# State space layer: B and C from one product, C copied by DMA, and dt in array quarters with one transpose

## The chip, the cores and the metric

The kernel runs on one core of one Trainium2 chip. The metric is the device time of one execution in microseconds (us); lower is better. Before the change three executions took 1665.72, 1667.54 and 1668.49 us; the median, 1667.54 us, is the time before.

The core has five engines that work side by side, each on its own list of instructions in order: TensorE (PE, matrix products and transposes; its weight loads are shown apart as PEld), VectorE (DVE), ScalarE (ACT), GpSimd (POOL) and SyncE (SP, here only an issuer of transfers). Transfers run on 16 DMA engines. Products go to PSUM, which has banks of 128 partitions by 512 float32, and are copied from there into SBUF.

## The reference

Two layers over x of 4 sequences, 1024 tokens, 256 features, all in float32. Layer 0 is a state space mixer and a feed-forward network, layer 1 a linear attention and a mixture of experts; each of the four parts ends in a residual sum and a layernorm. The part that the change touches is the projection of the state space mixer, cut from the reference:

```
def ssd_forward(x, W_xproj, dt_bias, A_log, D):
    dtBC = x @ W_xproj.T                       # 256 features -> 2 + 64 + 64
    dt = dtBC[..., :NHEADS]                    # one step size for each of 2 heads
    Bm = dtBC[..., NHEADS:NHEADS + D_STATE]    # D_STATE = 64
    Cm = dtBC[..., NHEADS + D_STATE:]
    dt = jax.nn.softplus(dt + dt_bias)
    A = -jnp.exp(A_log)
    Xh = x.reshape(b, T, NHEADS, HEADDIM) * dt[..., None]
    y = ssd_minimal_discrete(Xh, A * dt, Bm, Cm, T)    # B, C shared by both heads
    return y + x * D_full
```

The mixer itself weighs the products of C (of a later token) with B (of an earlier one) by a decay exp of the sum of A dt between the two, and multiplies the result with dt x. The kernel does this by tiles of 128 tokens and carries a state of 64 x 128 per head from tile to tile, which C reads (the reference computes a sequence at once; the result is the same).

## The kernel before

**Tiles and stages.** The 4096 tokens are eight blocks of 512: block i belongs to sequence i // 2, and an odd block continues its even one. Each block has four tiles of 128 tokens. x is loaded twice, as rows (x0 to x7, tokens on partitions) and turned (xt0 to xt7, features on partitions). `two_layers` (L74) is the whole kernel; `ssd_block` (L265) makes one block of the state space mixer, `ffn_block` (L418) one of the feed-forward network, `attn_front` and its fellows half a block of the attention, and shared and routed jobs the experts.

**One state space block.** `project(0)` (L272) multiplies xt with weights whose 128 columns are B (64), dt (2) and padding, so that bc0 has B on partitions 0 to 63 and dt on 64 and 65, with 512 tokens along; `project(1)` does it with C twice, so that bc1 has C on both halves of the partitions. Each is two products of 128x128 with 128x512 (the profile counts each of these instructions twice), and an ACT copy out of PSUM (L279). `steps` (L281) turns bc0 by four transposes (L285), copies B and dt (128 x 264) to dtb by ACT (L287), and computes the step sizes with a softplus in some twenty small DVE operations (L293 to L306) and one ACT exp (L295). The last of them gives a (L306). `sums` (L309) makes cumulative sums of a by three products with constant masks (L316) and their exp, and the first `shade` (L327): on POOL am (L332), the mask scaled by a, and bs (L334), B scaled by step and decay. `scores` (L336) multiplies B by C of each tile (L341; 64 partitions are contracted) and masks on DVE (L343). For each tile j, `weights(j)` (L347) makes the decays (product L350, exp L352) and weighs the scores (DVE L355); `step(j)` (L361) makes y (L371), the state's addition s (L380) and the reading of the old state by C (L385: head 0 with C and state on partitions 0 to 63, head 1 on 64 to 127), and DVE sums them up. After the fourth tile comes the layernorm.

**Who sets the order.** PE's order is fixed by a planner at build time: every stage is a `Task` (class at L231) with a cost, a rank, waits after other tasks, and PSUM banks of one of two pools (six banks for the state space and the attention, two for the feed-forward network). `trace_tasks` takes the task that can begin first and, of equals, that of lowest rank; its planned times decide the order alone, while on the chip each instruction runs when semaphores allow. The even blocks come first, the odd ones follow as their even ones end, and the feed-forward blocks fill the gaps in the order 0, 2, 1, 3 to 7. The other engines are ordered by the framework's scheduler. The tasks of the front part of a block are

```
t_b = Task(lambda: project(0), 1.8, r, [(before, 0.0)], 0, 1)
t_c = Task(lambda: project(1), 1.8, r + 0.02, [(t_b, 0.0)], 0, 1)
t_d = Task(steps, 0.5, r + 0.01, [(t_b, 1.7)], 0, 1)
t_c = Task(scores, 0.9, r + 0.02, [(t_c, 1.7)], 0, 1, 2.0)
t_u = Task(sums, 0.5, r + 0.03, [(t_d, 7.0)], 0, 1, 1.0)
```

**Loads.** SP issues the loads up to the router's weights ahead of anything else (L118 to L135): the projection's weights wx, xt0, small vectors, xt2, xt4, xt6, x0, x2, x4, x6, col, the feed-forward weights w1 and w2, then xt1, x1, xt3, x3 and so on, and the attention's weights; then zero fills of the routed slots (L1062). Transfers reuse a limited set of semaphores, so that an issue can wait for an earlier transfer with the same one.

Of the kernel before, what the change touches and what calls it, by code (L numbers as in the profile page):

```python
# [23 lines left out]
F32 = mybir.dt.float32  # L24
# [6 lines left out]
P = 128  # L31
NB, T, D = 4, 1024, 256
TB = 512
NT = TB // P
# [5 lines left out]
VW = 32  # L40
# [33 lines left out]
def two_layers(ctx: ExitStack, tc: tile.TileContext, x, xT, vecs, cols, wx, w1, w2, wqkv, wout, om, rw, moe, out):  # L74
# [29 lines left out]
    w2_sb = wkf.tile([P, HID0 // P, D], F32, name="w2_sb")  # L104
    ssd_pool = tc.tile_pool(name="l0s", bufs=1, side="right")
    wk0 = ssd_pool.__enter__()
    wx_sb = wk0.tile([P, KC, 2, P], F32, name="wx_sb")
    xts = [wk0.tile([P, KC, TB], F32, tag=f"xt{i // 2}", name=f"xt{i}", bufs=2) for i in range(NBLK)]
    attw_pool = tc.tile_pool(name="attw", bufs=1)
    wkw = attw_pool.__enter__()  # L110
# [152 lines left out]
    def ssd_block(i, wk):  # L263
# [6 lines left out]
        def small(tag):  # L270
            return sm.tile([P, NT, NH1], F32, tag=f"ssd{b}_{tag}", name=f"ssd_{tag}{i}")

        def project(s):

            ps = bank(f"ps_bc{i}_{s}", 0)
            for k in range(KC):
                nc.tensor.matmul(ps, wx_sb[:, k, s, :], xts[i][:, k, :], start=(k == 0), stop=(k == KC - 1))
            v.bc[s] = wk.tile([P, TB], F32, tag=f"bc{b}_{s}", name=f"bc{i}_{s}")
            nc.scalar.copy(v.bc[s], ps)  # L279

        def steps():  # L281

            ps = bank(f"ps_dtb{i}", 0)
            for j in range(NT):
                nc.tensor.transpose(ps[:, j * P : (j + 1) * P], v.bc[0][:, j * P : (j + 1) * P], ident)  # L285
            dtb = v.dtb = wk.tile([P, NT, NST + NH1], F32, tag=f"dtb{b}", name=f"dtb{i}")
            nc.scalar.copy(dtb, ps.rearrange("p (j n) -> p j n", j=NT)[:, :, : NST + NH1])  # L287

            z, e, w, w2, q, dt, a = v.chain = [small(t) for t in ("z", "e", "w", "w2", "q", "dt", "a")]
            bias = vec0[:, _VEC["dt_bias"]].unsqueeze(1).to_broadcast([P, NT, NH1])
            nc.vector.tensor_add(z, dtb[:, :, NST:], bias)  # L293
            nc.vector.scalar_tensor_tensor(e, z, -1.0, z, ALU.mult, ALU.max)
            nc.scalar.activation(e, e, AF.Exp, scale=-1.0)  # L295
            nc.vector.tensor_scalar_add(w, e, 2.0)
            nc.vector.reciprocal(w, w)
            nc.vector.tensor_mul(w, w, e)
            nc.vector.tensor_mul(w2, w, w)
            nc.vector.tensor_scalar_mul(q, w2, 1.0 / 17.0)  # L300
            for n in (15.0, 13.0, 11.0, 9.0, 7.0, 5.0, 3.0):
                nc.vector.scalar_tensor_tensor(q, q, 1.0 / n, w2, ALU.add, ALU.mult)
            nc.vector.scalar_tensor_tensor(q, q, 1.0, w, ALU.add, ALU.mult)
            nc.vector.tensor_scalar_max(z, z, 0.0)
            nc.vector.scalar_tensor_tensor(dt, q, 2.0, z, ALU.mult, ALU.add)
            nc.vector.tensor_mul(a, dt, neg_a.unsqueeze(1).to_broadcast([P, NT, NH1]))  # L306
# [20 lines left out]
        def shade(j):  # L327

            v.am[j] = wk.tile([P, NH1, P], F32, tag=f"am{b}", name=f"am{i}_{j}", bufs=2)
            v.bs[j] = wk.tile([P, NH1, NST], F32, tag=f"bs{b}", name=f"bs{i}_{j}", bufs=2)  # L330
            for h in range(NH1):
                nc.gpsimd.tensor_scalar_mul(v.am[j][:, h, :], mask_le, v.chain[6][:, j, h : h + 1])  # L332
            for h in range(NH1):
                nc.gpsimd.tensor_scalar_mul(v.bs[j][:, h, :], v.dtb[:, j, :NST], v.dts[:, j, h : h + 1])  # L334

        def scores():  # L336

            ps = bank(f"ps_sc{i}", 0)
            for j in range(NT):
                tok = slice(j * P, (j + 1) * P)  # L340
                nc.tensor.matmul(ps[:, tok], v.bc[0][:NST, tok], v.bc[1][:NST, tok], start=True, stop=True)  # L341
            v.sc = wk.tile([P, NT, P], F32, tag=f"sc{b}", name=f"sc{i}")
            nc.vector.tensor_mul(  # L343
                v.sc, ps.rearrange("p (j l) -> p j l", j=NT), mask_le.unsqueeze(1).to_broadcast([P, NT, P])
            )
# [15 lines left out]
        def step(j):  # L361


            state = states[b]
            tok = slice(j * P, (j + 1) * P)
            first, last = i % 2 == 0 and j == 0, i % 2 == 1 and j == NT - 1
            ps_y, ps_s = (bank(f"ps_{n}{i}_{j}", 0) for n in "ys")
            halves = [slice(h * NST, (h + 1) * NST) for h in range(NH1)]
            past = [ps_y[:, D : D + P], ps_s[:, P : 2 * P]]
            for h in range(NH1):  # L370
                nc.tensor.matmul(  # L371
                    ps_y[:, h * P : (h + 1) * P],
                    v.wt[j][:, h, :],
                    x_i[:, j, h * P : (h + 1) * P],
                    start=True,
                    stop=True,
                )
            if not last:
                for h in range(NH1):
                    nc.tensor.matmul(  # L380
                        ps_s[halves[h], :P], v.bs[j][:, h, :], x_i[:, j, h * P : (h + 1) * P], start=True, stop=True
                    )
            if not first:
                for h in range(NH1):
                    nc.tensor.matmul(past[h], v.bc[1][halves[h], tok], state[halves[h], :], start=True, stop=True)  # L385
            if not last:
                new = wk.tile([P, P], F32, tag=f"state{b}", name=f"state{i}_{j}", bufs=2)
                if first:
                    nc.vector.tensor_copy(new, ps_s[:, :P])
                else:  # L390
                    nc.vector.scalar_tensor_tensor(new, state, v.end[:, j : j + 1], ps_s[:, :P], ALU.mult, ALU.add)
                states[b] = new
            for h in range(NH1):
                xh = x_i[:, j, h * P : (h + 1) * P]
                nc.vector.scalar_tensor_tensor(
                    xh, xh, d_plus[:, h : h + 1], ps_y[:, h * P : (h + 1) * P], ALU.mult, ALU.add
                )
                if not first:
                    nc.vector.scalar_tensor_tensor(xh, past[h], v.ex[:, 0, j, h : h + 1], xh, ALU.mult, ALU.add)
            if j == NT - 1:  # L400
                layernorm(i, by_act=True)

        before = ssd_end.get(i - 1) if i % 2 else None
        r = b + 0.4 * (i % 2)
        t_b = Task(lambda: project(0), 1.8, r, [(before, 0.0)], 0, 1)
        t_c = Task(lambda: project(1), 1.8, r + 0.02, [(t_b, 0.0)], 0, 1)
        t_d = Task(steps, 0.5, r + 0.01, [(t_b, 1.7)], 0, 1)
        t_c = Task(scores, 0.9, r + 0.02, [(t_c, 1.7)], 0, 1, 2.0)
        t_u = Task(sums, 0.5, r + 0.03, [(t_d, 7.0)], 0, 1, 1.0)
        t_s = None  # L410
        for j in range(NT):
            s = r + 0.04 + 0.01 * j
# [787 lines left out]
def _layout(g):  # L1200
# [7 lines left out]

    w = _rows(g["L0_attn_W_xproj"].T)
    dt, bm, cm = w[:, :, :NH1], w[:, :, NH1 : NH1 + NST], w[:, :, NH1 + NST :]  # L1210
    pad = np.zeros((P, KC, P - NST - NH1), w.dtype)
    wx = np.stack([np.concatenate([bm, dt, pad], axis=2), np.concatenate([cm, cm], axis=2)], axis=2)

    def expert(w1, w3, w2):
        return np.concatenate([_rows(w1.T), _rows(w3.T), _rows(w2.T).reshape(P, 2, HID)], axis=1)
# [41 lines left out]
```

## Time and profile before

The profile is of one execution of 1667.01 us; the span from its first to its last instruction is 1665.3 us.

| | us | share of the span |
|---|---|---|
| profiled execution | 1667.01 | |
| its span | 1665.3 | |
| PE busy | 1530.3 | 92% |
| PE weight loads busy | 1000.9 | 60% |
| DVE busy | 745.2 | 45% |
| ACT busy | 606.0 | 36% |
| POOL busy | 479.5 | 29% |
| state space projection (L277) on PE | 31.6 | 2% |
| its four transposes per block (L285) on PE | 4.9 | 0.3% |
| ACT copies of bc (L279) and dtb (L287) | 9.2 and 3.0 | 0.7% |

The mean granted TensorE clock is 0.960 of full speed. Busy times of different engines overlap. The state space blocks lie in the first tenth of the span: the first product is at about 5 us, the last tile of block 7 at 164 us. A stretch with everything busy says nothing of which engine the others wait for; the waits and the stretches between them do. In rows of instructions, the columns are start, length, engine, line, operation, output<-inputs, shapes and count, and in brackets the idle time of the engine before and the one that ended it. In rows of groups, they are line, engine, operation, output<-inputs, shapes and count, then busy us and mean ns of one, then idle us before and who ended them.

### The profile page before, as it was taken

To read this page: it belongs to the slowest core of one execution; us is meant where nothing else is said; L and a number is where in the kernel's file an instruction comes from. 1 tells how busy PE (TensorE), PEld (TensorE's weight loads), DVE (VectorE), ACT (ScalarE), POOL (GpSimd) and SP (SyncE) were. 2 spreads that over 40 slices of the span, in tenths; PEclk is the share of its full clock that TensorE was granted. 3 is DMA by queue.
4 is the path that set the end of the run, shared out by engine and by line. 5 is a ranking of instruction groups with operands and counts; after the bars stand their busy time and mean duration, and the time that the engine had idled before them with its cause. 6 is when DMAs were issued, how large, how long until landed. Compare 5 with 4: busy or idle time off the path is not lost.

```text
span 1665.3 us, 25514 instructions
## 1 busy us (share of the span) xinstructions
PE 1530.3 (92%) x9680; PEld 1000.9 (60%) x9680; DVE 745.2 (45%) x2264; ACT 606.0 (36%) x1065; POOL 479.5 (29%) x509
## 2 busy tenths in 40 slices
PE   8999898989999989999999972989999999999887
PEld 5566565757676757657667641456666666665554
DVE  6877734756566538454544410112222222222665
ACT  2545463464635365354565200112222222221221
POOL 6623243443323434233322077030000000003541
PEclk9999999999999999999999995899999999999999
DMA  9400000000000002001000382031111111111331
GB/s 346 184 1 1 1 1 1 14 1 1 14 2 14 1 14 89 1 14 35 6 14 27 124 324 104 29 111 45 48 45 45 45 47 46 46 41 57 117 105 64
DMA packets 53207, 92.60 MB, mean 56 GB/s; under 512 B 6624, under 2 KB 37472, under 8 KB 51552
## 3 DMA queue, kind: packets, MB, share of 16 engines
q1 hardware_dynamic: 44496, 67.89, 11.5%
q0 software_dynamic: 6864, 19.41, 3.6%
q10 hardware_dynamic: 1728, 3.67, 0.6%
q8 instruction: 80, 1.31, 0.3%
q14 instruction: 39, 0.32, 0.1%
HBM read 52.93 MB, written 38.01 MB: 55 GB/s over the span
## 4 chain that ended last, share of the span: by engine, by line
PE 71%; DVE 12%; ACT 8%; issue 4%; POOL 3%; DMA 1%; SPq 1%; DVEq 0%; ACTq 0%; POOLq 0%
PE ps_ge L944 15%; PE ps_g L882 12%; PE ps_ye L966 7%; PE ps_e L900 7%; PE ps_f L442 5%; PE ps_h L430 5%; PE ps_sc L600 3%; PE ps_o L636 3%; PE ps_gT L959 2%; PE ps_qk L486 2%; PE ps_k L622 1%; PE ps_v L511 1%; PE ps_p L548 1%; ACT L433 1%; PE ps_xe L935 1%
## 5 line engine op out<-in xcount | busy, mean ns | idle before, releaser
L944 PE MATMUL ps_ge<-w,xeT 128*128 x568 | 258.2, 598 | 0.7 <-ACT xeT L937 0.6
L882 PE MATMUL ps_g<-xTs,w 128*128 128x512 f32 x512 | 229.6, 602 | 6.1 <-ACT sl L890 6.1
L993 POOL DMA_INDIRECT y<-yg,slot x64 | 62.8, 981 | 453.5 <-ACT sl L890 404.0
L900 PE MATMUL ps_e<-w,gT 128*128 128x256 f32 x512 | 132.1, 407 | 58.9 <-issue 46.7
L882 PEld LDWEIGHTS ps_g<-xTs,w 128*128 128x128 f32 x512 | 96.6, 192 | 120.1 <-issue 108.2
L944 PEld LDWEIGHTS ps_ge<-w,xeT 128*128 128x128 f32 x568 | 103.3, 192 | 104.8 <-issue 103.8
L900 PEld LDWEIGHTS ps_e<-w,gT 128*128 128x128 f32 x512 | 102.3, 203 | 88.0 <-issue 59.6
L430 PE MATMUL ps_h<-xT,w_sb 128*128 128x512 f32 x256 | 129.6, 650 | 22.3 <-ACT hT L433 12.9
L954 DVE TENSOR_TENSOR ge<-se,ps_ge 128x512 f32<-128x512 f32 x71 | 48.8, 687 | 222.9 <-PE ps_ge L944 222.9
L966 PE MATMUL ps_ye<-w2e,geT 128*128 x568 | 134.4, 380 | 0.0
L891 DVE TENSOR_TENSOR gT<-sl,ps_g 128x512 f32<-128x512 f32 x64 | 43.9, 686 | 196.5 <-PE ps_g L882 159.9
L442 PE MATMUL ps_f<-w_sb,hT 128*128 128x256 f32 x512 | 118.1, 385 | 1.6 <-ACT hT L433 1.6
L966 PEld LDWEIGHTS ps_ye<-w2e,geT 128*128 128x128 f32 x568 | 102.5, 190 | 12.3 <-ACT ye L974 0.8
L442 PEld LDWEIGHTS ps_f<-w_sb,hT 128*128 128x128 f32 x512 | 96.6, 192 | 17.4 <-issue 3.1
L961 DVE COPY geT<-ps_gT 128x512 f32<-128x512 f32 x71 | 49.1, 691 | 114.4 <-PE ps_gT L959 114.4
L430 PEld LDWEIGHTS ps_h<-xT,w_sb 128*128 128x128 f32 x256 | 49.9, 205 | 80.4 <-issue 54.6
L612 DVE TENSOR_TENSOR sc<-ps_sc,mask_le 128x512 f32<-128x512 f32 x96 | 62.6, 684 | 62.0 <-PE ps_sc L600 53.0
L952 ACT ACTIVATE se<-ps_ge 128x512 f32<-128x512 f32 x71 | 42.4, 597 | 127.1 <-PE ps_ge L944 127.1
L561 POOL TENSOR_SCALAR qf<-qf,csq 128x512 f32<-128x512 f32 x32 | 50.2, 1570 | 116.4 <-ACT qf L559 115.1
L890 ACT ACTIVATE sl<-ps_g 128x512 f32<-128x512 f32 x64 | 37.7, 594 | 125.8 <-PE ps_g L882 100.2
L854 POOL DMA_INDIRECT xg<-x,slot x64 | 61.7, 964 | 66.7 <-DMA w<-in_moe 47.5
L610 POOL TENSOR_TENSOR sc<-sc,mask_le 128x512 f32<-128x512 f32 x32 | 41.1, 1283 | 133.5 <-ACT sc L609 133.4
(235 smaller groups left out, 2600.6 us busy)
## 6 DMA issues: line engine op xcount, KB each, us to landing
xe<-xg SPq DMA_DIRECT2D x71, 128.0 KB
yg<-ye SPq DMA_DIRECT2D x71, 128.0 KB
xg<-zero SPq DMA_DIRECT2D x35, 256.0 KB
w<-in_moe SPq DMA_DIRECT2D x8, 1024.0 KB
xt<-in_xT SPq DMA_DIRECT2D x8, 512.0 KB
x<-in_x SPq DMA_DIRECT2D x8, 512.0 KB
td<-xTr SPq DMA_DIRECT2D x16, 256.0 KB
w2e<-in_moe SPq DMA_DIRECT2D x8, 512.0 KB
```

The costliest lines, as they stand in the source:

```text
L430: nc.tensor.matmul(ps, w1_sb[:, k, m * P : (m + 1) * P], v.xT[:, k, :], start=(k == 0), stop=(k == KC - 1))
L442: nc.tensor.matmul(v.ps[:, j % 2, :], v.hT[:, m, j * P : (j + 1) * P], w2_sb[:, m, :], start=(m == 0), stop=(m == HID0 // P - 1),)
L561: nc.gpsimd.tensor_scalar_mul(f, f, csq)
L600: nc.tensor.matmul(ps[s][:, r * P : (r + 1) * P], kf[rows, r, q, tok], qf[rows, r, q, tok], start=True, stop=True)
L612: nc.vector.tensor_mul(t_s, ps_s, mask)
L636: nc.tensor.matmul(ps_o[c * VW : (c + 1) * VW, g * P : (g + 1) * P], v1[:, j, h, :] if own else kv[:, h, :], sc[j][f // 4][:, 4 * s + f % ...
L854: ins = nc.gpsimd.indirect_dma_start(out=xg, out_offset=bass.IndirectOffsetOnAxis(ap=slot[:, n, t : t + 1], axis=0), in_=xs[i][:, j, :], i ...
L882: nc.tensor.matmul(ps[s], w[e][:, 2 * s + k, m * P : (m + 1) * P], xT[i][:, k, :], start=(k == 0), stop=(k == KC - 1),)
L900: nc.tensor.matmul(ps, gT[i, e][:, m, j * P : (j + 1) * P], w2e[:, m, :], start=(e == 0 and m == 0), stop=(e == NSH - 1 and m == HID // P ...
L944: nc.tensor.matmul(pg[a], xeT[s][:, k, :], w13[:, bass.ds(e * (4 * HID) + (2 * a + k) * HID, HID)], start=(k == 0), stop=(k == KC - 1),)
L966: nc.tensor.matmul(ps[:, :D], geT[s][:, m, :], w2[:, bass.ds(of[s] * (2 * HID) + m * D, D)], start=(m == 0), stop=(m == HID // P - 1),)
L993: nc.gpsimd.indirect_dma_start(out=y, out_offset=None, in_=yg, in_offset=bass.IndirectOffsetOnAxis(ap=slot[:, n, t : t + 1], axis=0),)
```

## The change

The weights wx become B (64 columns), C (64) and dt padded to 32 (VW). `project` then is one product with B on partitions 0 to 63 and C on 64 to 127, one ACT copy, and a DMA, issued by ACT, that copies C (64 x 512, 128 KB) to a tile on partitions 0 to 63. `scores` and head 0's reading of the state take that copy; head 1's takes C where it lies. dt has a product of its own, `project_dt`: for each of the four tiles of 128 tokens, the 32 columns of weights give 32 rows of PSUM, so that the four tiles fill the 128 partitions; it is copied by ACT (128 x 128) and turned by a single transpose in `steps`, from which DVE reads dt in PSUM. B is turned on its own, 64 rows at a time, in `turn_b`, and copied by ACT (128 x 256) for `bs`. dt's task comes before the product of B and C in the planner, and the waits of the tasks are changed; the planner's order of other tasks follows from these. Block 0's issue of the copy, for instance, stands behind the exp of its softplus on ACT in the order that is built.

```diff
--- before.py
+++ after.py
@@ -104,7 +104,7 @@
     w2_sb = wkf.tile([P, HID0 // P, D], F32, name="w2_sb")
     ssd_pool = tc.tile_pool(name="l0s", bufs=1, side="right")
     wk0 = ssd_pool.__enter__()
-    wx_sb = wk0.tile([P, KC, 2, P], F32, name="wx_sb")
+    wx_sb = wk0.tile([P, KC, P + VW], F32, name="wx_sb")
     xts = [wk0.tile([P, KC, TB], F32, tag=f"xt{i // 2}", name=f"xt{i}", bufs=2) for i in range(NBLK)]
     attw_pool = tc.tile_pool(name="attw", bufs=1)
     wkw = attw_pool.__enter__()
@@ -270,27 +270,52 @@
         def small(tag):
             return sm.tile([P, NT, NH1], F32, tag=f"ssd{b}_{tag}", name=f"ssd_{tag}{i}")
 
-        def project(s):
-
-            ps = bank(f"ps_bc{i}_{s}", 0)
+        def project():
+
+            ps = bank(f"ps_bc{i}", 0)
             for k in range(KC):
-                nc.tensor.matmul(ps, wx_sb[:, k, s, :], xts[i][:, k, :], start=(k == 0), stop=(k == KC - 1))
-            v.bc[s] = wk.tile([P, TB], F32, tag=f"bc{b}_{s}", name=f"bc{i}_{s}")
-            nc.scalar.copy(v.bc[s], ps)
+                nc.tensor.matmul(ps, wx_sb[:, k, :P], xts[i][:, k, :], start=(k == 0), stop=(k == KC - 1))
+            v.bc = wk.tile([P, TB], F32, tag=f"bc{b}", name=f"bc{i}")
+            nc.scalar.copy(v.bc, ps)
+            v.c = [wk.tile([NST, TB], F32, tag=f"c{b}", name=f"c{i}"), v.bc[NST:]]
+            nc.scalar.dma_start(out=v.c[0], in_=v.bc[NST:])
+
+        def project_dt():
+
+            ps = bank(f"ps_dt{i}", 0)[:, :P]
+            for j in range(NT):
+                for k in range(KC):
+                    nc.tensor.matmul(
+                        ps[j * VW : (j + 1) * VW, :],
+                        wx_sb[:, k, P:],
+                        xts[i][:, k, j * P : (j + 1) * P],
+                        start=(k == 0),
+                        stop=(k == KC - 1),
+                    )
+            v.dT = wk.tile([P, P], F32, tag=f"dT{b}", name=f"dT{i}")
+            nc.scalar.copy(v.dT, ps)
+
+        def turn_b():
+
+            ps = bank(f"ps_b{i}", 0)
+            for j in range(NT):
+                nc.tensor.transpose(
+                    ps[:, j * NST : (j + 1) * NST], v.bc[:NST, j * P : (j + 1) * P], ident[:NST, :NST]
+                )
+            v.b = wk.tile([P, NT, NST], F32, tag=f"b{b}", name=f"b{i}")
+            nc.scalar.copy(v.b.rearrange("p j n -> p (j n)"), ps[:, : NT * NST])
 
         def steps():
 
-            ps = bank(f"ps_dtb{i}", 0)
-            for j in range(NT):
-                nc.tensor.transpose(ps[:, j * P : (j + 1) * P], v.bc[0][:, j * P : (j + 1) * P], ident)
-            dtb = v.dtb = wk.tile([P, NT, NST + NH1], F32, tag=f"dtb{b}", name=f"dtb{i}")
-            nc.scalar.copy(dtb, ps.rearrange("p (j n) -> p j n", j=NT)[:, :, : NST + NH1])
+            ps = bank(f"ps_z{i}", 0)[:, :P]
+            nc.tensor.transpose(ps, v.dT, ident)
+            turned = ps.rearrange("p (j n) -> p j n", n=VW)[:, :, :NH1]
 
 
 
             z, e, w, w2, q, dt, a = v.chain = [small(t) for t in ("z", "e", "w", "w2", "q", "dt", "a")]
             bias = vec0[:, _VEC["dt_bias"]].unsqueeze(1).to_broadcast([P, NT, NH1])
-            nc.vector.tensor_add(z, dtb[:, :, NST:], bias)
+            nc.vector.tensor_add(z, turned, bias)
             nc.vector.scalar_tensor_tensor(e, z, -1.0, z, ALU.mult, ALU.max)
             nc.scalar.activation(e, e, AF.Exp, scale=-1.0)
             nc.vector.tensor_scalar_add(w, e, 2.0)
@@ -331,14 +356,14 @@
             for h in range(NH1):
                 nc.gpsimd.tensor_scalar_mul(v.am[j][:, h, :], mask_le, v.chain[6][:, j, h : h + 1])
             for h in range(NH1):
-                nc.gpsimd.tensor_scalar_mul(v.bs[j][:, h, :], v.dtb[:, j, :NST], v.dts[:, j, h : h + 1])
+                nc.gpsimd.tensor_scalar_mul(v.bs[j][:, h, :], v.b[:, j, :], v.dts[:, j, h : h + 1])
 
         def scores():
 
             ps = bank(f"ps_sc{i}", 0)
             for j in range(NT):
                 tok = slice(j * P, (j + 1) * P)
-                nc.tensor.matmul(ps[:, tok], v.bc[0][:NST, tok], v.bc[1][:NST, tok], start=True, stop=True)
+                nc.tensor.matmul(ps[:, tok], v.bc[:NST, tok], v.c[0][:, tok], start=True, stop=True)
             v.sc = wk.tile([P, NT, P], F32, tag=f"sc{b}", name=f"sc{i}")
             nc.vector.tensor_mul(
                 v.sc, ps.rearrange("p (j l) -> p j l", j=NT), mask_le.unsqueeze(1).to_broadcast([P, NT, P])
@@ -382,7 +407,7 @@
                     )
             if not first:
                 for h in range(NH1):
-                    nc.tensor.matmul(past[h], v.bc[1][halves[h], tok], state[halves[h], :], start=True, stop=True)
+                    nc.tensor.matmul(past[h], v.c[h][:, tok], state[halves[h], :], start=True, stop=True)
             if not last:
                 new = wk.tile([P, P], F32, tag=f"state{b}", name=f"state{i}_{j}", bufs=2)
                 if first:
@@ -402,11 +427,12 @@
 
         before = ssd_end.get(i - 1) if i % 2 else None
         r = b + 0.4 * (i % 2)
-        t_b = Task(lambda: project(0), 1.8, r, [(before, 0.0)], 0, 1)
-        t_c = Task(lambda: project(1), 1.8, r + 0.02, [(t_b, 0.0)], 0, 1)
-        t_d = Task(steps, 0.5, r + 0.01, [(t_b, 1.7)], 0, 1)
-        t_c = Task(scores, 0.9, r + 0.02, [(t_c, 1.7)], 0, 1, 2.0)
-        t_u = Task(sums, 0.5, r + 0.03, [(t_d, 7.0)], 0, 1, 1.0)
+        t_d = Task(project_dt, 0.5, r, [(before, 0.0)], 0, 1)
+        t_b = Task(project, 1.8, r, [(t_d, 0.0)], 0, 1)
+        t_d = Task(steps, 0.15, r + 0.01, [(t_d, 1.7), (t_b, 0.0)], 0, 1)
+        t_t = Task(turn_b, 0.3, r + 0.02, [(t_b, 1.7)], 0, 1)
+        t_c = Task(scores, 0.9, r + 0.02, [(t_b, 4.7), (t_t, 0.0)], 0, 1, 2.0)
+        t_u = Task(sums, 0.5, r + 0.03, [(t_d, 6.5), (t_t, 1.5)], 0, 1, 1.0)
         t_s = None
         for j in range(NT):
             s = r + 0.04 + 0.01 * j
@@ -1208,8 +1234,7 @@
 
     w = _rows(g["L0_attn_W_xproj"].T)
     dt, bm, cm = w[:, :, :NH1], w[:, :, NH1 : NH1 + NST], w[:, :, NH1 + NST :]
-    pad = np.zeros((P, KC, P - NST - NH1), w.dtype)
-    wx = np.stack([np.concatenate([bm, dt, pad], axis=2), np.concatenate([cm, cm], axis=2)], axis=2)
+    wx = np.concatenate([bm, cm, np.pad(dt, ((0, 0), (0, 0), (0, VW - NH1)))], axis=2)
 
     def expert(w1, w3, w2):
         return np.concatenate([_rows(w1.T), _rows(w3.T), _rows(w2.T).reshape(P, 2, HID)], axis=1)
```

## The prediction

> **What bounds the kernel now.** I read the page's slices first, then the busy time of the engines by stage, then groups by shape, and last single stretches. All times are us, ns where marked. In the slices (tenths busy in 40 equal parts of the span):
>
> ```profile
> PE   8999898989999989999999972989999999999887
> ...
> DMA  9400000000000002001000382031111111111331
> ```
>
> TensorE is the bound nearly everywhere, and the loads fill the DMA engines only in the first slices, which is where the change works. The busy time by stage (stretch, length, then PE, weight loads, DVE, ACT and POOL with counts, granted clock, DMA share, GB/s):
>
> ```profile
> 20.00:45.00 25.00, 24.83 (x149) 17.38 (x148) 23.49 (x109) 6.96 (x19) 23.33 (x45) 1.00 1.03 384
> 45.00:70.00 25.00, 22.33 (x125) 14.22 (x124) 22.84 (x122) 14.45 (x29) 15.58 (x27) 1.00 0.69 254
> ```
>
> PE leads, but DVE (23.49 and 22.84 of 25) and POOL (23.33 in the first) are hardly behind, and the DMA engines are full until 45 and later. So PE time that is saved here is a gain only until DVE's chain or a transfer is late. The waits that PE has show where that is: its two long ones are at block 1's cumulative sums and ahead of a first FFN product:
>
> ```profile
> 56.16 0.36 PE L316 MATMUL ps_cum<-ssd_a,mask_le 128*128 128x8 f32 x2 [1.22 <-DVE ssd_a L306]
> ...
> 137.04 5.37 PE L430 MATMUL ps_h<-xT,w_sb 128*128 128x512 f32 x8 [1.75 <-DVE xT L197]
> ```
>
> The bracket is idle time and who ended it. After the 1.75 the eight products take 5.37 where such a pair takes about 3.45 elsewhere: a pause also cost some 1.8 of slow clock (granted clock 0.95 in 130 to 165).
>
> **The change on PE.** Today a block's projection and transposes are one stretch:
>
> ```profile
> 41.98 0.27 PE L385 MATMUL ps_s<-state,bc 64*128 64x128 f32 x1
> 42.18 3.70 PE L277 MATMUL ps_bc<-xt,wx_sb 128*128 128x512 f32 x8
> 45.72 0.60 PE L285 MATMUL ps_dtb<-ident,bc 128*128 128x128 f32 x4
> 46.16 0.61 PE L371 MATMUL ps_y<-x,wt 128*128 128x128 f32 x4
> ```
>
> From start to start: 45.72-42.18 = 3.54 for both products, 46.16-45.72 = 0.44 for four transposes; 3.98 per block. Afterwards: one product, 3.54/2 = 1.77. The dt product (eight 128x32 products of 128 columns, 16 instructions in the profile's count) has the form of the router's logits:
>
> ```profile
> 310.65 0.67 PE L741 MATMUL ps_l<-xTr,rw_sb 128*32 128x128 f32 x16
> 311.25 0.50 PE L548 MATMUL ps_p<-qkT,om_sb 32*128 32x256 f32 x4
> ```
>
> 311.25-310.65 = 0.60. One transpose is 0.44/4 = 0.11 at that pitch, 0.27 (what one transpose of that line lasts by its record) if it stands alone; 0.15 taken. Four half transposes (64 rows by 128) are not in the trace: from 0.30 (a little under the whole ones) to 0.55; 0.45 taken, their nearest row. Sum 1.77+0.60+0.15+0.45 = 2.97, so 1.0 per block is saved, 8.0 over eight blocks.
>
> A rule speaks against the dt part: the Trainium skill's "TensorEngine Tiling (Array Packing)", Key Properties, says that changing the array's tiling mode drains TensorE, and dt adds some three changes per block. If each cost what a lone transpose lasts over its pitch (0.27-0.11 = 0.16), that is 0.5 per block and 4.0 in all: half the saving. The row says otherwise: in the stretch above, 64x128 is followed by 128x128 at 42.18, 0.20 after the start before it, as within one kind, and the 0.60 above is bounded by two changes. I take 0.2 in all, 4.0 as the end.
>
> **The change on ACT, DVE, POOL.** The evictions:
>
> ```profile
> L279 ACT COPY bc<-ps_bc 128x512 f32<-128x512 f32 x16 | 9.2, 584 | 18.9 <-PE ps_bc L277 18.7
> ...
> L287 ACT COPY dtb<-ps_dtb 128x264 f32<-128x264 f32 x8 | 3.0, 380 | 1.5 <-PE ps_dtb L285 1.5
> ...
> L749 ACT COPY lT<-ps_l 128x128 f32<-128x128 f32 x8 | 2.1, 260 | 3.5 <-PE ps_l L741 3.5
> ```
>
> Before 2 x 0.584+0.380 = 1.55 per block; after 0.584 + 0.26 (dT) + 0.38 (b) + 0.33 for issuing the copy = 1.55. ACT's share is unchanged, 0. DVE loses nothing and gains nothing: the softplus chain's 20-odd small operations (0.17 to 0.20 each, some 4 us) stay, reading from PSUM. What changes is when it starts: dt no longer waits for a product with B. For block 0, z starts at 11.32 today; xt0 lands 0.27 earlier (wx is 96 KB smaller, at about 350 GB/s), and 1.77-0.60, a copy 0.12 shorter and the transposes put it at about 9.6. POOL's bs wants the new b copy as well, which comes some 2 after z and before dts; nothing. Two table loads fewer in the built order (80 to 78, 1.28 each) lie on ACT, which has slack; nothing.
>
> **The copy of C.** It adds a transfer, and three waits. The scores wait for it on PE, with everything behind them in PE's written order. Its issue waits on ACT: block 0's behind the exp of the softplus chain, block 4's for a semaphore that x0's load used, block 6's for block 0's copy; dT2's and bc2's evictions are queued behind the issue for block 0, so PE's z2 and b2 too. On SP, where loads go out in order, the loads of x1, x5 and x7 now wait for the copies of blocks 2, 4 and 6, and all later loads and zero fills behind them; some 2.6 MB (7 us) in flight ahead, and data first needed after 50, cover that; with the cover gone it costs what the copy is late. By counting instructions along the new order I find the slack from issue to need: block 0 issued 10.4, needed 14.5 (4.1); block 2 4.6; block 4 6.1; block 6 2.9. How long does a copy take?
>
> ```profile
> 1093.25 0.33 ACTq L912 DMA_DIRECT2D sd<-so  x1
> ...
> 1095.85 0.59 POOL L1151 DMA_DIRECT2D part<-sd  x1 [55.31 <-DMA sd<-so]
> ```
>
> ```profile
> 10.15 2.03 SPq L125 DMA_DIRECT2D col<-in_cols  x1
> ...
> 18.09 0.15 DVE L1050 TENSOR_SCALAR fcap<-col 128x1 f32<-128x1 f32 x1 [0.95 <-DMA col<-in_cols]
> ```
>
> On ACT's queue 256 KB landed within 2.6 with the engines free. Under the load a tiny transfer took up to 7.9, but it stood on SP's queue behind megabytes. The Trainium skill's "DMA: Bandwidth & Descriptors", Issuing engines are not separate DMA queues, says that transfers of all issuers run on the same 16 engines and interleave; so the copy does not wait for the whole of SP's queue, but neither is it alone, with a share of 1.03. By the 2.6 row nothing is lost; by the 7.9 row (7.9-4.1)+(7.9-2.9) = 8.8. I take 3.5, nearer the first (the queue is the same): 0 + 0.6 = 0.6 lost.
>
> **Where the saving goes.** PE alone: -8.0. Given back: (1) The first four blocks bring PE 4.0 ahead by 42. Block 1's chain is not ahead as much: its exp stands behind two table loads on ACT (exp at 49.72 today, with no earlier place in the new order), and DVE is full; I put its last value at about 55 against 55.87, PE at its cumulative sums at 52: a wait of 3.1 for 1.22, +1.9. (2) Block 3's the same, +2.1. (3) After such waits the clock drops as at 137.04: +1.7. (4) At block 7, b7 and cum7 wait 2.7 to 3.4 in place of 1.75 with its slow clock of 1.8: +0.5, its ends -0.8 and +1.0. (5) An FFN piece (3.45) that now comes ahead of block 7's last step makes that later, but DVE and ACT find less after it; at the attention's next product 0, ends -0.6 and +3.45. (6) Mode changes 0.2, the copies 0.6. Sum -8.0+1.9+2.1+1.7+0.5+0.2+0.6 = -1.0. From about 190 on PE's order is that of before, so a shift there stays to the end.
>
> The profiled execution is 1667.0 (span 1665.3, 1.7 around it); so 1666.0 for it, and as the median of the runs is 0.5 above it, **1666.5**.
>
> **The rivals.** *Faster:* PE is the bound as the slices say, DVE's chain comes earlier with dt first, and the waits grow by 2 at most: -6 to -8, about 1660. For it: PE is busy 33.25 of 35 and 59.87 of 60 in the stages after 70. Against: 23.49 of 25 on DVE.
> *Slower:* the copies land late. One mechanism: under a DMA share of 1.03 a copy of C takes over 4.1 in block 0 and over 2.9 in block 6, and every us beyond delays the scores, PE behind them, and through PE's order DVE and POOL. At 7.9 it loses 8.8 in place of 0.6: -1.0+8.2 = +7.2, 1674.7. It decides from about 5.2, where the loss (3.4) eats the gain. Col's row and SP's issue of 2.03 speak for it, ACT's own queue against.
> *Nothing moves:* DVE and POOL set the time to 70 altogether, whatever PE saves, and later waits take the rest: 0, 1667.5.
>
> **How the numbers follow.** About 0.2%, 3.3 us, is what a measurement of this kernel can tell from no change. The likeliest case, with small gains and losses around -1.0, gets 0.42 (own range 1662.5 to 1670.5: faster 0.07, same 0.28, slower 0.07), the faster rival 0.21, the slower one 0.25, nothing moves 0.12 (same 0.09, slower 0.03). Faster 0.28, same 0.37, slower 0.35. The range takes in both rivals: 1659.5 (all of the saving but 0.5) to 1675 (copies as late as col's row).
>
> **What would show it.** PE from dt to b at 2.97 per block in sum; dt's sixteen at 0.60. Scores that PE waits for with the copy of C as releaser: none but block 6's, under 1. Cumulative sums of blocks 1 and 3 with DVE's ssd_a as releaser, 3 and 2 long. If the scores of blocks 0 to 6 wait over 3 together, the slower rival is right; if PE's waits before 165 grow by under 2, the faster one. Wrong I would also be if the planner's later order (the FFN piece) costs its 3.45, or a late load of x1 holds block 1.

## The result and the profile after

The changed kernel takes 1678.77 us (median of five, 1677.89 to 1680.69) where the kernel before takes 1665.72 (median of five on the same chip): a ratio of 1.0078, with a 95% interval of 1.0062 to 1.0094. It is 13 us slower. The forecast was 1666.5 with a range to 1675.0, so the time lies outside it, on the side of the slower rival.

The span went from 1665.3 to 1677.1. First the slices (tenths of busy time; for PEclk the granted clock in tenths of full speed; the first slice is 0 to 42, the second 42 to 84):

```profile
PE   7999878999899989999999982889999999999887
...
PEclk7899999999999999999999995899999999999999
DMA  9600000000000002000000282031111111111332
```

Before, the first 24 slices of PEclk were all 9. Now the first two are 7 and 8, so TensorE ran at a lower clock just where the change is. The busy time by stage shows it closer (stretch, length, then PE, weight loads, DVE, ACT and POOL, then granted clock, DMA share, GB/s):

```profile
20.00:45.00 25.00, 22.08 (x105) 16.09 (x104) 15.37 (x73) 4.57 (x15) 18.68 (x37) 0.66 0.98 343
45.00:70.00 25.00, 21.80 (x167) 15.54 (x166) 23.11 (x126) 9.87 (x22) 9.43 (x20) 0.95 0.49 170
70.00:130.00 60.00, 60.00 (x312) 41.69 (x311) 46.91 (x208) 30.92 (x53) 27.80 (x52) 0.91 0.20 72
130.00:165.00 35.00, 32.09 (x156) 20.00 (x155) 22.44 (x111) 19.50 (x31) 10.08 (x17) 0.90 0.02 4
```

Where the first row had 149 products at clock 1.00 before, it now has 105 at 0.66. DVE, which was busy 23.49 of these 25 us, is now busy 15.37: it is not the bound there, and most of what it waits for is TensorE (5.4 us; 3.6 for ACT). The clock is either full or half in the trace, so 2 x (1-0.66) x 25 = 17 us of this stage were at half clock; the other rows give 2.5, 10.8 and 7.0. Together 37 us up to 165, against 3.5 before (0.95 in 130 to 165). Where TensorE is the bound, each us at half clock costs up to half a us.

What TensorE waits for up to 165 (engine, tile, line, and who ended the wait: us in total, times, longest):

```profile
PE ps_cum L341 <- DVE ln_s L179: 2.9, 1, 2.9
PE ps_cum L341 <- DVE ssd_a L331: 2.7, 1, 2.7
PE ps_sc L366 <- DVE ssd_q L327: 2.3, 1, 2.3
PE ps_sc L366 <- DMA c<-bc: 2.0, 2, 1.4
PE ps_b L302 <- ACT bc L279: 0.2, 1, 0.2
PE ps_s L405 <- ACT dec L377: 0.2, 1, 0.2
```

That is 10.3, against 4.6 before (without the first load in both). The cumulative sums of blocks 1 and 7 wait for DVE's softplus chain, and the scores of blocks 0, 2 and 6 for the copy of C. A row names what ended last by the profile, which need not be an input. The first one names ln_s, an operation of a layernorm, but the sums read ssd_a, the end of the softplus chain, which DVE makes among its layernorm work just before them:

```profile
67.43 0.16 DVE L331 TENSOR_TENSOR ssd_a<-ssd_dt,neg_a 128x8 f32<-128x8 f32 x1
67.73 0.56 PE L341 MATMUL ps_cum<-ssd_a,mask_le 128*128 128x8 f32 x2 [2.89 <-DVE ln_s L179]
```

The third one names ssd_q, which is no input of the scores; their one late input is the copy. Its issues on ACT's queue and the scores that use it:

```profile
10.54 0.51 ACTq L281 DMA_DIRECT2D c<-bc  x1
13.16 0.47 ACTq L281 DMA_DIRECT2D c<-bc  x1
...
27.50 0.47 ACTq L281 DMA_DIRECT2D c<-bc  x1
```

```profile
17.05 1.13 PE L366 MATMUL ps_sc<-c,bc 64*128 64x128 f32 x8 [1.38 <-DMA c<-bc]
...
20.70 2.04 PE L366 MATMUL ps_sc<-c,bc 64*128 64x128 f32 x8 [0.61 <-DMA c<-bc]
...
33.90 2.04 PE L366 MATMUL ps_sc<-c,bc 64*128 64x128 f32 x8 [2.30 <-DVE ssd_q L327]
```

From issue to use: 6.5, 7.5 and 6.4. And the same eight products take 1.13 at full clock but 2.04 from 20.70 on: the clock has fallen. The work itself is what was forecast; one stretch with two odd blocks' front parts:

```profile
54.75 0.67 PE L288 MATMUL ps_dt<-xt,wx_sb 128*32 128x128 f32 x16
55.34 1.98 PE L277 MATMUL ps_bc<-xt,wx_sb 128*128 128x512 f32 x4
57.17 0.27 PE L311 MATMUL ps_z<-ident,dT 128*128 128x128 f32 x1
57.27 0.61 PE L396 MATMUL ps_y<-x,wt 128*128 128x128 f32 x4
...
61.12 0.46 PE L302 MATMUL ps_b<-ident,bc 64*128 64x64 f32 x4
61.51 0.33 PE L311 MATMUL ps_z<-ident,dT 128*128 128x128 f32 x1
```

By the starts, dt takes 0.59, B and C 1.83, the transpose of dt 0.10, the four of B 0.39: 2.91 for a block that took 3.98.

Two marks show when the time is lost. The attention's first feature product starts at 194.3 before and at 209.7 after, 15.5 later: the whole loss and more lies ahead of it. TensorE's order behind it is the same in both kernels. The first router logits are 15.3 later, the last ones (942.5 and 953.1) only 10.6; the end 11.8. What is made up goes with less half clock behind the mark, 124.6 us in place of 131.3; why it is less was not studied.

### The profile page after: what moved, and what is told of

Same layout as the page of the kernel before. It is cut to its first block, busy times and chain, and to the rows that moved or that the text cites. A ratio compares the mean times of both kernels' runs of the same rounds, so it can differ in the third digit from the quotient of the medians.

```text
span 1677.1 us, 25731 instructions
## 1 busy us (share of the span) xinstructions
PE 1533.4 (91%) x9784; PEld 1007.5 (60%) x9784; DVE 742.3 (44%) x2264; ACT 600.8 (36%) x1063; POOL 478.0 (29%) x509
## 4 chain that ended last, share of the span: by engine, by line
PE 74%; DVE 11%; ACT 8%; issue 4%; POOL 2%; DMA 1%; SPq 0%; DVEq 0%; ACTq 0%
PE ps_ge L970 15%; PE ps_g L908 11%; PE ps_ye L992 7%; PE ps_e L926 6%; PE ps_f L468 6%; PE ps_h L456 5%; PE ps_sc L626 3%; PE ps_o L662 3%; PE ps_gT L985 2%; PE ps_qk L512 2%; PE ps_seg L375 1%; PE ps_k L648 1%; DVE x L218 1%; PE ps_v L537 1%; ACT L459 1%
```

## The experiments

Runs were made on chips that differ in speed (the kernel before takes 1608 on some, 1662 to 1666 on others), so each is given as a ratio to the kernel before on the same chip. The theory at the start was A: the waits let the clock fall, and the fallen clock is the larger part. Its rivals were B, that the short products of the change bring the clock down whatever the waits, and C, that DVE and POOL set this stage.

**Filling the waits.** An idle product before a waiting one keeps TensorE at work:

```diff
+        def fill(ps, n):
+            for _ in range(n):
+                nc.tensor.matmul(ps, ident, xts[i][:, 0, :], start=True, stop=True)
...
             ps = bank(f"ps_sc{i}", 0)
+            fill(ps, {0: 3, 2: 2, 6: 5}.get(i, 0))
...
             n8 = NT * NH1
+            fill(ps, {1: 6, 7: 6}.get(i, 0))
```

> The changed kernel with idle products put on TensorE ahead of the scores of blocks 0, 2 and 6 (3, 2 and 5 products of 128x128 with 128x512, into the bank that the scores then overwrite) and ahead of the cumulative sums of blocks 1 and 7 (6 each). They wait for nothing late, so they fill the waits with work. Theory A (the clock): the waits themselves are a third of the loss, and the larger part is that TensorE's clock is at half for some 37 us after them before 165; filled waits keep it at full, half clock before 165 falls to 10 us or less, and the time falls by 10 to 14 from the changed kernel's 1678.8, to about 1666. Theory B (the form of the work: short products and array quarters count as little work, whatever the waits): the half clock stays at 30 us or more, the time at 1677 to 1681. Theory C (DVE and POOL set the stage): the clock recovers, but the time falls by under 3.

Measured: ratio 1.0077 (1.0048 to 1.0105), 1617.47. The half clock before 165 was down to 3.4, as A has it, but the time was not: I had taken one such product for 0.43, and it takes 0.89. The 22 of them are 19.6, where waits of 9.9 were to be filled. The clock follows the filling; the price can't be read from this run alone.

**C of the even blocks by a product.** The copy is replaced by a second product and eviction, in the same order:

```diff
-            nc.scalar.dma_start(out=v.c[0], in_=v.bc[NST:])
+            if i % 2 == 1:
+                nc.scalar.dma_start(out=v.c[0], in_=v.bc[NST:])
+                return
+            ps = bank(f"ps_c{i}", 0)[:NST]
+            for k in range(KC):
+                nc.tensor.matmul(ps, wx_sb[:, k, NST:P], xts[i][:, k, :], start=(k == 0), stop=(k == KC - 1))
+            nc.scalar.copy(v.c[0], ps)
```

> The changed kernel with the copy of C of the four even blocks replaced by a second product of C's 64 columns and an ACT copy; odd blocks keep the transfer. TensorE has 4 x 1.77 = 7.1 more. Theory A (late copies and the half clock after them): the waits ahead of the scores (some 4.3) and the half clock between 20 and 42 (17, so 8 of time) go: 1678.8+7.1-4.3-8 = 1673.6, the granted clock of 20 to 45 above 0.95. Theory B (form of the work): half clock stays, 1682 to 1686. Theory C (other engines): waits of the same size with DVE or POOL as releaser appear, 1678 to 1680.

Measured: 1.0127 (1.0096 to 1.0158), 1626.78. The waits for the copy are gone, and the half clock up to 165 is 17 us in place of 37, but the cumulative sums now wait more:

```profile
PE ps_cum L347 <- DVE ssd_a L337: 5.8, 3, 2.7
...
PE ps_cum L347 <- DVE ssd_w L327: 2.5, 1, 2.5
```

They are 8.3, where the changed kernel has 5.6 for the sums and 4.3 for copies, and the time is longer by about the 7.1 that was added. So the late copies were not the loss by themselves: behind them the softplus chain was late as well. A's number was missed.

**The loads held back.** SP's loads from the FFN weights on wait until block 6's copy is issued:

```diff
             nc.scalar.dma_start(out=v.c[0], in_=v.bc[NST:])
+            if i == 6:
+                nc.scalar.copy(w1_sb[:1, 0, :1], v.bc[:1, :1])
+                with tc.manual_schedule(engines={mybir.EngineType.SP}):
+                    rest_of_loads()
```

`rest_of_loads` holds the issues from w1 to rw and the zero fills, which are taken from their old place.

> The changed kernel with all loads from the FFN weights on (and the zero fills) held on SP until block 6's copy of C is issued (one element of the first is written by ACT after it); nothing else is changed. If the load on the DMA engines is what makes the copies late (theory A), the copies of blocks 2, 4 and 6 land in 2.5 to 3.5 in place of 6.4 to 7.5, TensorE waits under 1 in all for the scores, the clock in 20 to 45 is above 0.95, and the time falls by 9 to 12, to about 1668. If a copy on ACT's queue takes that long whatever the load, the landing stays at 6 or more and the time at 1678 or above. If held loads are late for block 1 or the FFN, a wait on DMA appears after 45.

Measured: 1.0092 (1.0062 to 1.0123), 1621.56: no gain. Block 0's copy still met the even blocks' loads and landed 6.4 after its issue (wait 1.3). Block 6's was issued at 26.60 with the engines idle, and its scores ran at 30.63 without a wait for it: at most 4.0, against 6.4. So the load is what makes the copy late, but it isn't what the time turned on. What stayed was the half clock, 38 us of it by the stages. This run also decides a part of the question between A and B. The busy time in steps of 2 us:

```profile
26.00:28.00 2.00, 2.00 (x15) 1.81 (x15) 0.87 (x4) 0.92 (x3) 1.45 (x4) 1.00 0.13 30
28.00:30.00 2.00, 2.00 (x14) 1.66 (x12) 1.26 (x6) 0.95 (x3) 2.00 (x5) 0.79 1.04 245
30.00:32.00 2.00, 2.00 (x8) 1.37 (x7) 1.64 (x9) 0.48 (x2) 2.00 (x4) 0.50 1.00 406
```

TensorE is busy all the time and waits for nothing, and its clock falls to half. The rows of these 4 us:

```profile
25.77 0.28 PE L348 MATMUL ps_cum<-ssd_a,mask_le 128*128 128x8 f32 x2
25.91 0.37 PE L348 MATMUL ps_cum<-ssd_a,mask_gt 128*128 128x8 f32 x2
26.14 0.37 PE L348 MATMUL ps_cum<-ssd_a,ones 128*128 128x8 f32 x2
26.43 1.16 PE L373 MATMUL ps_sc<-c,bc 64*128 64x128 f32 x8
27.52 0.70 PE L382 MATMUL ps_seg<-am,mask_gt 128*128 128x256 f32 x2
28.05 0.27 PE L318 MATMUL ps_z<-ident,dT 128*128 128x128 f32 x1
28.26 0.46 PE L309 MATMUL ps_b<-ident,bc 64*128 64x64 f32 x4
```

All are short (8 to 128 columns a time, but for one), and some use half of the array's rows or columns. So I worked out a use of the array for each step of 3.4 us (the trace's changes of clock fall on such steps): columns streamed, at the 0.43 per 512 of the long products, times the share of the rows and columns used. In the step ahead of the changed kernel's first fall it is 0.32 (with 0.6 of the wait of 1.38 in it; the wait of 0.61 comes after the fall), in the stretch just shown 0.33, ahead of the kernel before's only fall 0.26. The changed kernel's second fall also comes without a wait, at a use of 0.33:

```profile
26.67:30.08 3.41, 3.41 (x27) 2.90 (x25) 1.86 (x7) 1.51 (x4) 2.68 (x7) 1.00 1.05 377
30.08:33.50 3.42, 1.51 (x5) 0.79 (x4) 2.65 (x13) 0.67 (x3) 3.42 (x7) 0.50 1.06 332
```

Theory D is that this use is what the clock follows, so that waits and short products add up.

**The kernel before, filled.** Three idle products ahead of block 1's cumulative sums and four ahead of block 2's first FFN product:

```diff
+            fill(ps, {1: 3}.get(i, 0))
...
                 ps = bank(f"ps_h{i}_{m}", 1)
+                for _ in range(4 if i == 2 and m == 0 else 0):
+                    nc.tensor.matmul(ps, ident, w1_sb[:, 0, :TB], start=True, stop=True)
```

> The kernel before with idle products ahead of block 1's cumulative sums (3) and ahead of the first FFN product of block 2 (4), where it waits 1.22 and 1.75. Theory A: the half clock of 3.4 at 137 goes, and the time falls by 1.5 to 2. Theory B: no change, or 0.5 to 1 more.

Measured: 1.003 (1.0015 to 1.0045). No half clock was left before 165; but here too 6.2 of idle products stood where 3.0 was waited, so the run says little of the price.

**The changed kernel again, and fills that fit.**

> The changed kernel as it is, for the chip of this call. Theory D, from the traces so far: the half clock is set by the array's use in each 3.4 us (columns streamed, weighed by the share of the array's rows and columns that a product uses): windows under some 0.4 are followed by half clock. The changed front part has more of them, by its waits and by its short products. All theories: a ratio to before of 1.006 to 1.009, half clock before 165 of 30 to 40 us.

Measured: 1.0095 (1.0076 to 1.0114), 41 us of half clock before 165 by the stages. The fitted fill differs from the first one in its numbers alone:

```diff
-            fill(ps, {0: 3, 2: 2, 6: 5}.get(i, 0))
+            fill(ps, {0: 1, 6: 2}.get(i, 0))
...
-            fill(ps, {1: 6, 7: 6}.get(i, 0))
+            fill(ps, {4: 1, 1: 3, 7: 3}.get(i, 0))
```

> The changed kernel with idle products fitted to its waits: each lasts 0.89 (in the first attempt 22 of them, 19.6, stood where 9.9 was waited; that is 9.7 too many). Now 1 ahead of block 0's scores, 1 ahead of block 4's cumulative sums, 2 ahead of block 6's scores, 3 each ahead of the cumulative sums of blocks 1 and 7: 8.9. Theory D: half clock before 165 at 7 or less, the first product of the attention's features at 194 to 198 in place of 209.7, and the ratio at 0.998 to 1.001, 11 to 15 us under the changed kernel. If the clock is not the larger part of the loss but the waits are: within 4 us of the changed kernel.

Measured: 1.0074 (1.0055 to 1.0093), 1674.68; four runs from 1668.84 to 1675.10. The profiled one is the fastest: 10 us of half clock, and the attention's first feature product at 203.8, which is 7.9 earlier than in the changed kernel on this chip (211.7), but not at 194 to 198. D's number was missed: in the median filled waits bring 4, at best 10, of 16. The trace shows why. The idle products did not take the waits' place: up to that product TensorE still waits 10.6, against 13.0 in the changed kernel on this chip (without the first load), and 8.9 of idle products come on top. So this run does not say that the clock was worth little.

**The planner's waits.** What all of them have in common is that TensorE's written order puts an instruction ahead of the time at which its input is there. The planner counts 4.7 from the product of B and C to the scores (measured in the loaded stage: 0.6 for the eviction, then 6.4 to 7.5 from the issue to the use) and 6.5 from the transpose of dt to the cumulative sums (measured for block 1: from 57.17 to 67.73). With both set longer:

```diff
-        t_c = Task(scores, 0.9, r + 0.02, [(t_b, 4.7), (t_t, 0.0)], 0, 1, 2.0)
-        t_u = Task(sums, 0.5, r + 0.03, [(t_d, 6.5), (t_t, 1.5)], 0, 1, 1.0)
+        t_c = Task(scores, 0.9, r + 0.02, [(t_b, 8.0 if i % 2 == 0 else 4.7), (t_t, 0.0)], 0, 1, 2.0)
+        t_u = Task(sums, 0.5, r + 0.03, [(t_d, 6.5 if i % 2 == 0 else 10.0), (t_t, 1.5)], 0, 1, 1.0)
```

> The changed kernel with the planner's waits set as measured: scores of even blocks 8.0 after the product in place of 4.7, cumulative sums of odd blocks 10.0 after the transpose of dt in place of 6.5. Other work is thereby put ahead of them; no instruction is added. Theory D: TensorE waits under 3 in all before the last state space tile, half clock before 165 at 14 or less, ratio 0.996 to 1.001. If DVE's chain sets this part, other waits of the same size replace them: ratio 1.005 to 1.009.

Measured: 1.0000 (0.9989 to 1.0011), 1663.08: the same instructions in another order are 15.4 faster than the changed kernel on this chip. The waits up to 165, after the first load:

```profile
PE ps_y L396 <- DVE wt L380: 1.9, 1, 1.9
PE ps_txT L195 <- ACT x L213: 1.5, 4, 1.0
PE ps_sc L366 <- DMA c<-bc: 0.7, 1, 0.7
```

4.1 in place of 10.3 (8.0 on this chip), and 17 us of half clock in place of 41. That the loss came with the order, and not with the new instructions, is shown, since these are the same. Which moves in the order did it is not shown: the two numbers move many tasks at once.

**Each of the two alone.**

> Of the two planner waits of the run that came back to the time before, only the one of odd blocks' cumulative sums (10.0 after the transpose of dt in place of 6.5); scores stay at 4.7. If the loss lay mostly in the odd blocks' softplus chain, its waits (2.9 and 2.7) and their half clock (20): the ratio at 1.002 to 1.005, the half clock between 68 and 82 gone. If mostly in the late copies: 1.007 to 1.009.

> The other wait alone: scores of even blocks 8.0 after the product of B and C in place of 4.7; cumulative sums stay at 6.5. If the late copies are the larger part: ratio 1.002 to 1.005, waits for copies under 1 and less half clock between 20 and 42; waits for the cumulative sums of blocks 1 and 7 stay. If the smaller part: 1.006 to 1.008.

Measured: 1.0083 (1.0054 to 1.0113) for the cumulative sums alone, 1.0075 (1.0044 to 1.0106) for the scores alone: neither brings anything. The parts don't add. In the first the copies are still late (4.6 in three waits), and the new order has a wait of 4.8 at an FFN product:

```profile
PE ps_h L456 <- DVE xT L197: 4.8, 1, 4.8
PE ps_sc L366 <- DMA c<-bc: 4.6, 3, 2.6
PE ps_y L396 <- DVE wt L380: 3.1, 1, 3.1
```

In the second, the copies are in time, the 2.9 at the cumulative sums stays, and an FFN product waits 4.6. Which of the two the loss "belongs" to has no answer: with one late input gone, another is next.

**The copy of C alone.** The kernel before, whose scores and first head read C from a copy of the high half:

```diff
             nc.scalar.copy(v.bc[s], ps)
+            if s == 1:
+                v.c = [wk.tile([NST, TB], F32, tag=f"c{b}", name=f"c{i}"), v.bc[1][NST:]]
+                nc.scalar.dma_start(out=v.c[0], in_=v.bc[1][NST:])
...
-        t_c = Task(scores, 0.9, r + 0.02, [(t_c, 1.7)], 0, 1, 2.0)
+        t_c = Task(scores, 0.9, r + 0.02, [(t_c, 4.7)], 0, 1, 2.0)
```

> The kernel before with one part of the change: its two products and four transposes stay, but the low half's C is taken from a copy by transfer of the high half, issued by ACT, and the scores wait 4.7 after the product of C in the planner. No product is saved, so TensorE's work is that of before. If late copies by themselves are the loss, the scores wait 3 to 6 in all, the half clock before 165 is 15 or more, and the ratio 1.005 to 1.008. Theory D: the long products keep the array's use up, half clock at 10 or less, ratio 1.000 to 1.003.

Measured: 1.0060 (1.0040 to 1.0079). D's number was missed: the copy with its planner wait costs 10 us on top of the work of before, though the products are the long ones and the half clock is 14 us only. Again it isn't the copy alone:

```profile
PE ps_cum L319 <- DVE ln_s L180: 4.2, 1, 4.2
PE ps_sc L344 <- DMA c<-bc: 2.6, 2, 2.0
PE ps_y L374 <- DVE wt L358: 1.6, 1, 1.6
```

The scores' later place moves other tasks, and a cumulative sum then waits 4.2.

**A version that beats both.** The planned waits, and four idle products where windows of low use were left:

```diff
+            fill(ps, {2: 1, 4: 1, 3: 2}.get(i, 0))
```

The line stands in `scores`; both planner waits are as in the run above.

> The version with both planner waits, and four idle products (0.89 each) where its windows of low use were: 1 ahead of block 2's scores, 1 ahead of block 4's, 2 ahead of block 3's. If the clock is worth what its share says, the remaining 17 of half clock before 165 fall to 7 or less and the ratio is 0.996 to 0.999. If filling costs as much as it brings: 0.999 to 1.003.

Measured: 0.9970 (0.9958 to 0.9982), 1602.08 against 1607.94. Up to 165, TensorE waits 1.5 beside its first load, and the half clock is 3.5 (0.93 in 45 to 70, 1.00 elsewhere); in 20 to 45 it is busy 25.00 of 25. The four products, 3.6 of idle work, bring about 0.3%, 5 us, by the ratios of the two runs.

The same two means in the kernel before:

```diff
-        t_u = Task(sums, 0.5, r + 0.03, [(t_d, 7.0)], 0, 1, 1.0)
+        t_u = Task(sums, 0.5, r + 0.03, [(t_d, 7.0 if i % 2 == 0 else 10.0)], 0, 1, 1.0)
```

> The kernel before with the same wait for odd blocks' cumulative sums (10.0 in place of 7.0). If a planner wait as measured is worth something of itself, the kernel before gains as well: its waits of 1.2 and 1.75 go, ratio 0.996 to 0.999. If it was fitted already: 0.999 to 1.003.

Measured: 0.9998 (0.9985 to 1.0011). With fitted fill (1 ahead of block 1's sums, 2 ahead of the FFN product) instead:

> The kernel before with idle products fitted to its own two waits (1 of 0.89 ahead of block 1's cumulative sums, where it waits 1.22; 2 ahead of the first FFN product of block 2, where it waits 1.75; the first attempt had 3 and 4). If the version with planned waits and fill is faster only because filled waits keep the clock up, the kernel before gains as much from its own: ratio 0.996 to 0.998. If that gain belongs to the change, the kernel before gains at most the half clock of 3.4: 0.998 to 1.001.

Measured: 0.9996 (0.9984 to 1.0008), without any half clock before 165. Neither of the two alone gains the kernel before anything (both together were not run), so the 0.3% of the other version are most likely the change's, given an order that suits it. The attention's first feature product agrees: 189.6 there, 194.5 in the kernel before with fitted fill (on another chip).

**Does the transfer pay, once planned?** The planned version with C of the even blocks by a product:

> The version with both planner waits (ratio 1.000), with C of the four even blocks made by a second product in place of the transfer: 7.1 more on TensorE, no copy under the load. If, once the order gives the copy time, the transfer is worth what it saves: ratio 1.002 to 1.005. If the late copies still cost in the planned version: 0.997 to 1.000.

Measured: 1.0029 (1.0010 to 1.0047). It is 0.29% slower than the planned version with the copy (1.0000), some 4.8 of the 7.1 that it adds. With time in the order, the late copy is hidden.

## Why the prediction was wrong

- **The saving on TensorE** was right: 2.97 forecast, 2.91 measured, dt 0.60 and 0.59. The Trainium skill's "TensorEngine Tiling (Array Packing)" (Key Properties) says that a change of tiling mode drains TensorE; no lost time for it shows in the steps of 0.59, 1.83, 0.10 and 0.39 from start to start, and the 0.2 taken for all of it was enough. What the short and narrow products did cost came by another way, the clock.
- **The landing of the copy** was wrong: 3.5 taken, 6.4 to 7.5 measured under load, at most 4.0 without. The prediction chose ACT's row of 2.6 with idle engines as the nearer one, because the queue was the same; the nearer one was col's 7.9, because the load was the same. The sentence of "DMA: Bandwidth & Descriptors" (Issuing engines are not separate DMA queues) was weighed and given too little weight: with a DMA share of 1.03 a transfer shares the engines with all that is under way. It cost 4.3 of waits where 0.6 was forecast. The forecast's own end of 8.8 was low as well, since it counts blocks 0 and 6 alone; block 2, with a slack of 4.6, waited too (0.61).
- **Giving back, (1) and (4)**, were right as waits: 2.89 at block 1's cumulative sums (3.1 forecast), 2.72 and 0.19 at block 7 (2.7 to 3.4). The +0.5 of (4) does not follow from its figures, though: 2.7 to 3.4 less 1.75 and 1.8 is below zero, and the 6.8 us of half clock behind this wait have no term of their own. **(2)** was wrong: block 3's sums didn't wait, probably since block 1's wait had already let them catch up. **(5)** was low: between 165 and the first feature product TensorE waits 4.9 in place of 2.4, where 0 was forecast (3.45 at its end).
- **(3) is the step that failed**: "after such waits the clock drops as at 137.04: +1.7". It counted one fall of 3.4 us for one place. Measured: 37 us at half clock up to 165 in place of 3.5. At 0.40 us for each (worked out in the next point) to 0.5, that is 14 to 17, eight to ten times the term. I had tied it to the long waits at the cumulative sums alone, and gave the waits for copies, and the short products, no clock at all.
- **The sum** can be closed from the sixteen traces. Take the time of the attention's first feature product, and subtract the first load, TensorE's waits over 0.15, 0.89 for each idle product, 7.1 for a second product of C and 3.45 where an FFN pair has moved ahead of it. What is left is 178.8, less 8.3 where the change is in, plus 0.40 for each us at half clock: within 1.4 in fifteen runs, and 2.2 in the kernel before with the longer planner wait. (These three numbers are an estimate, fitted to the runs. The half clock here takes in the start, 3.0 to 6.2 us from the first product to the trace's first record of the clock; block 0's product of B and C took 3.62 in it, where later ones take 1.98.) From before to after, waits grow from 7.0 to 15.2 and half clock from 6.4 to 48.7: -8.3 + 8.2 + 16.9 = +16.8, against 15.5 measured. By this estimate the waits ate the saving, and the clock is the loss. In the fitted fill, waits and idle products together grew by 6.5 over the changed kernel, which took back half of the 13 that its clock brought.
- **The slower rival** had late copies right (decided from some 5.2 of landing), and fell 4 short (1674.7) since it had no clock in it either. But they weren't the whole cause: without the copies under load (C by a product) the changed order was as slow. Below the numbers lies one omission. I asked for each wait whether the input is late, and took the planner's order as given; the planner's constants for the new tasks, 4.7 and 6.5, against the measured 7.0 to 8.1 and 10.6, were there to be compared.
- Right on the side: the loads of x1 to x7 that wait for copies on SP cost nothing (x7's went out at 33.78 in place of 23.96, and no product waited for one).

## What to carry to other kernels

Where a written order fixes an engine, check every planned wait of a new task against a duration from the trace taken under the same load: a transfer issued on an idle queue still waits on busy DMA engines (6.4 to 7.5 us here, at most 4.0 with idle ones). A change that replaces long products with short or narrow ones lowers the array's use even where TensorE stays busy, so sum up the clock by stage, not only the time saved. And when one late input is mended, look at once for the next: here two mended together brought 15 us, and each alone none.

## What was not expected of the hardware

The clock goes with how much of the array is used, not only with whether TensorE is busy. Over 16 traces and 638 windows of 3.4 us at full clock up to 165, with the use worked out as above: all 21 windows with a use up to 0.30 were followed by half clock, of those from 0.31 to 0.45 twelve were and 22 not, and of the 583 above none. Two of the twelve are the stretches shown in which TensorE waited for nothing. Columns alone, without the shares of rows and columns, sort the windows far worse: falls come up to 0.89, and 239 windows at or below that were not followed by one (21, with the shares, at or below 0.45). The way back is harder: no window at half clock with a use under 0.6 (of what half clock can do) was followed by full clock. The Trainium skill's "TensorE: Matmul & The Clock Gate" (Part 1) tells of idle and busy windows of about 3.4 us and two rates; the runs agree with both, and add that a window can be busy and still count as idle. That the use is the cause is argued from these windows and from the fills, after which 0 to 3.4 us of half clock before 165 were left in four runs and 10 in the fifth; it wasn't isolated by a run of its own.
